# All-rows work of layer 0 gathered in two gaps of each tile

## The chip, the cores and the metric

The kernel runs on one core of a Trainium2 chip. The metric is the device time of one execution in microseconds (us); the kernel before takes 2685.39 us (median of 3 runs, 2684.89 to 2687.76). All times below are in us. The engines are TensorE (PE; PEld are its weight loads), VectorE (DVE), ScalarE (ACT), GpSimd (POOL) and the queue that starts transfers (SP).

## The reference, cut to what matters

The input x is 4 images of 128 channels and 64 x 64 positions, in float32. Two layers run over the N = 4096 positions of each image:

```
# layer 0: attention without a mask, heads of 64 channels for q and k
xf = group_norm(x).reshape(b, 128, N)
q = Wq @ xf + bq;  k = Wk @ xf + bk;  v = Wv @ xf + bv      # q, k: 64 x N, v: 128 x N
x = x + v @ softmax(q.T @ k).T
# layer 1: causal attention over tokens, then a recurrent network
t = tokens(x);  u = layer_norm(t)
t = t + softmax(causal(u Wq.T (u Wk.T).T / sqrt(128))) (u Wv.T)
t = t + ffn(layer_norm(t))
```

The ffn projects with W, normalises over all tokens and runs a recurrence through time. The change doesn't touch it.

## The kernel before

An image is called a batch in the code (B = 4). Its 4096 query positions form NQ = 8 tiles of QT = 512. All batches go one after the other; in each, the 8 tiles of layer 0 come first, then the 8 tiles of layer 1. A tile is worked off in units. A unit is 256 key positions, as two halves of 128, against the tile's 512 queries. A tile of layer 0 has 16 units; tile c of layer 1 has 2(c + 1), since later keys are masked.

A unit has three parts. `score` (L408) multiplies K by Q on TensorE into a PSUM pair `ps` (L428) and takes the exponential on ScalarE into `s` (L441), or, for the first unit of a tile, straight into `total`, which the profile calls `tot`. `product` (L443) multiplies `s` by V on TensorE and accumulates in PSUM, `av` (L457), and adds `s` to `total` on VectorE (L475). The loop at L496 issues the scores of unit i + 1, then a `turn` of queued jobs, then the products of unit i. TensorE so has the exponential of one unit to wait for while it does the scores of the next.

In layer 0, q and k have 64 rows. K and Q are stored twice, in rows 0 to 63 and 64 to 127, and the two halves of a unit run side by side in two halves of the TensorE array. The products too are split into two sums of 64 rows each, `av0` and `av1`. The profile shows such matmuls as 64*128. Layer 1 and all other work use all 128 rows (128*128). "All-rows work" below means matmuls of 128 rows that are put between the units of layer 0. They are:

- `pq` of `prep0` (L317): the projection that gives Q of the next tile, copied out by ScalarE (L321);
- `pz` of `end` (L361): a matmul with `blocks` that sums, over partitions, the `part` that VectorE has made of `total` (L351 to L356). Its reciprocal (L363) and a transpose on VectorE (L365) scale the products (L367), and X is updated (L370);
- `pt` and `pb` of `layernorm` (L157): four transposes of a finished tile of X (L161), copied out by ScalarE (L163), statistics on VectorE (L167, L169), a power on GpSimd (L155), normalisation on VectorE into the V of layer 1 (L174), and four transposes back (L180), copied into the K of layer 1 (L181);
- `pq` and `pz`, `pm`, `px` of `prep1` and `sample` (L338, L234): Q of the first tile of layer 1, and one sampled score per batch that sets the shift of the exponential.

When a tile of layer 0 or the last of layer 1 is done, its sums are copied out of PSUM (`acc`, L469: one half by ScalarE, one by VectorE), and the next tile's first product waits for these copies, for its `av` uses the same banks.

What runs between the units is decided by a list of jobs. A job is a generator that yields between its steps; `turn` (L225) makes one step of each of the first two jobs. `end` of a tile and `prep` of the next are put at the head, norms and the norms and projections for the ffn (`wx`, L383: `pt_f`, `pb_f`, `pw`) at the tail. In layer 0 this gives, per tile, a gap with `pq` and `pz`, one with `pt` and one with `pb`, each two units after the one before. The norm of tile c is queued as soon as X of that tile is updated, and so runs in tile c + 1. A part of the last tile's work runs in the first units of layer 1. The order on each engine is that in which instructions are issued, with small shifts: on VectorE the sums of a tile stand ahead of the copy of `acc`.

PSUM for all-rows work comes from `ps_m`, two buffers that are used in turn. `s` tiles come from `sp`, four buffers.

Of the kernel before, what the change touches and what calls it, by code (L numbers as in the profile page):

```python
# [64 lines left out]
def fast(  # L65
# [13 lines left out]
    NQ = N // QT  # L79
# [110 lines left out]
    def residual(b, tag):  # L190

        T[b] = kv.tile([P, N], F32, tag=tag, name=f"T_{b}")
        nc.sync.dma_start(out=T[b], in_=D[b])

    with ExitStack() as actx:
# [22 lines left out]
        jobs = deque()  # L218

        def queue(steps):  # L220
            job = Job(steps)
            jobs.append(job)
            return job
# [8 lines left out]
        norms, ends, preps, feeds = {}, {}, {}, {}  # L232
# [93 lines left out]
        def norm1(b, c):  # L326

            if c == 0:
                K[1, b] = kv.tile([P, N], F32, tag="K1", name=f"K1_{b}")
                V[1, b] = kv.tile([P, NB, C], F32, tag="V1", name=f"V1_{b}")  # L330
            yield from layernorm(
                X[:, b, ts(c, QT)], tmp, small, ps_m, f"1_{b}_{c}",
                V[1, b][:, 4 * c : 4 * c + 4, :], K[1, b][:, ts(c, QT)],
            )
            if c == 0:
                preps[1, b, 0] = queue(prep1(b, 0))

        def prep1(b, c):  # L338
            pq = ps_m.tile([P, QT], F32, tag="m", name=f"pq1_{b}_{c}")
            nc.tensor.matmul(pq, lhsT=A1, rhs=K[1, b][:, ts(c, QT)], start=True, stop=True)  # L340
            Q[1, b, c] = qp.tile([P, QT], F32, tag="q1", name=f"q1_{b}_{c}")
            nc.scalar.copy(Q[1, b, c], pq)
            yield
            if c == 0:
                yield from sample(1, b)

        def end(layer, b, c, av, total):

            name = f"{layer}_{b}_{c}"
            both = total[:, 0, :]  # L350
            nc.vector.tensor_tensor(both, both, total[:, 1, :], ALU.add)  # L351

            zt = tmp.tile([P, QT // R, R], F32, tag="zt", name=f"zt_{name}")
            nc.vector.transpose(zt.rearrange("p j a -> p (j a)"), both)  # L354
            part = small.tile([P, QT // R], F32, tag="part", name=f"part_{name}")
            nc.vector.tensor_reduce(part, zt, AX.X, ALU.add)  # L356
            if len(av) == 2:
                nc.vector.tensor_tensor(av[0], av[0], av[1], ALU.add)
            yield
            pz = ps_m.tile([P, QT // R], F32, tag="m", name=f"pz_{name}")  # L360
            nc.tensor.matmul(pz, lhsT=blocks, rhs=part, start=True, stop=True)  # L361
            r = sums[:, (layer * B + b) * NQ + c, :]
            nc.vector.reciprocal(r, pz)  # L363
            rt = tmp.tile([P, QT], F32, tag="rt", name=f"rt_{name}")
            nc.vector.transpose(rt.rearrange("p (j a) -> p j a", a=R), r.unsqueeze(2).to_broadcast([P, QT // R, R]))  # L365
            u = one.tile([P, QT], F32, tag="u", name=f"u_{name}")
            nc.vector.tensor_tensor(u, av[0], rt, ALU.mult)  # L367
            dst = X[:, b, ts(c, QT)]
            if layer == 0:
                nc.vector.scalar_tensor_tensor(dst, u, gn[b]["bv"], dst, ALU.add, ALU.add)  # L370
                norms[b, c] = queue(norm1(b, c))
                yield
                return
            yield
            yield
            po = ps_m.tile([P, QT], F32, tag="m", name=f"po_{name}")
            nc.tensor.matmul(po, lhsT=W1v, rhs=u, start=True, stop=True)  # L377
            nc.vector.tensor_tensor(dst, dst, po, ALU.add)  # L378
            nc.sync.dma_start(out=D[b][:, ts(c, QT)], in_=dst)
            queue(wx(b, c))  # L380
            yield
# [16 lines left out]
        units = []  # L398
# [9 lines left out]
        def score(i):  # L408
            layer, b, c, u, n = units[i]
            t = layer, b, c  # L410
            if u == 0:
                if layer == 0 and c == 0:
                    for job in feeds[b]:
                        job.complete()
                if layer == 1:
                    ends[0, b, c].complete()
                    norms[b, c].complete()
                if t not in preps:
                    preps[t] = queue((prep1 if layer else prep0)(b, c))
                preps[t].complete()  # L420
                totals[t] = tot.tile([P, 2, QT], F32, tag="total", name=f"tot_{layer}_{b}_{c}")
            s = totals[t] if u == 0 else sp.tile([P, 2, QT], F32, tag="s", name=f"s_{i}")
            exps[i] = s
            first = [columns(layer, c, u, h) for h in range(2)]
            ps = ps_pair.tile([P, 2, QT], F32, tag="pair", name=f"ps_{i}")
            for h in range(2):
                rows = slice(0, P) if layer else ds(h * CQ, CQ)
                nc.tensor.matmul(  # L428
                    ps[:, h, first[h] :], lhsT=K[layer, b][rows, ts(2 * u + h, P)],
                    rhs=Q[t][rows, first[h] :], start=True, stop=True,  # L430
                )
            if layer and u >= 2 * c:
                for h in range(2):
                    edge = ps[:, h, ds(first[h], P)]
                    nc.vector.tensor_tensor(edge, edge, mask, ALU.add)  # L435
                if u == 0:
                    nc.gpsimd.memset(s[:, 1, : first[1]], 0.0)
            for a in [(slice(None), slice(0, QT))] if first[1] == 0 else [
                (h, slice(first[h], QT)) for h in range(2)
            ]:  # L440
                nc.scalar.activation(s[:, *a], ps[:, *a], AF.Exp, bias=shift[layer, b])  # L441

        def product(i):  # L443
            layer, b, c, u, n = units[i]
            t = layer, b, c

            halves = [slice(0, P)] if layer else [ds(k * CQ, CQ) for k in range(2)]
            if u == 0:
                avs[t] = [
                    ps_av.tile([P, QT], F32, tag=f"av{(c + k) % 2}", name=f"av{k}_{layer}_{b}_{c}")  # L450
                    for k in range(len(halves))
                ]
            s, total, av = exps.pop(i), totals[t], avs[t]
            first = [columns(layer, c, u, h) for h in range(2)]
            for h in range(2):
                for rows, acc in zip(halves, av):
                    nc.tensor.matmul(  # L457
                        acc[:, first[h] :], lhsT=V[layer, b][rows, 2 * u + h, :],
                        rhs=s[rows, h, first[h] :],
                        start=u == 0 and h == 0, stop=u == n - 1 and h == 1,  # L460
                    )
            if u == n - 1 and (layer == 0 or c == NQ - 1):

                acc = [
                    pool.tile([P, QT], F32, tag=f"acc{k}", name=f"acc{k}_{i}")
                    for k, pool in zip(range(len(av)), (tmp, one))
                ]
                for cp, dst, src in zip((nc.scalar.copy, nc.vector.tensor_copy), acc, av):
                    cp(dst, src)  # L469
                av = acc  # L470
            if u:
                for a in [(slice(None), slice(0, QT))] if first[1] == 0 else [
                    (h, slice(first[h], QT)) for h in range(2)
                ]:
                    nc.vector.tensor_tensor(total[:, *a], total[:, *a], s[:, *a], ALU.add)  # L475
            if u == n - 1:
                ends[t] = Job(end(layer, b, c, av, total))
                jobs.appendleft(ends[t])
            if u == 0:
                if layer == 1 and c == 3 and b + 1 < B:  # L480
                    start_batch(b + 1)
                if layer == 1 and c == 3 and b == B - 1:
                    residual(0, "K0")
                    residual(1, "V0")
                following = layer, b, c + 1
                if c + 1 < NQ and (layer == 0 or (b, c + 1) in norms and norms[b, c + 1].done):
                    preps[following] = Job((prep1 if layer else prep0)(b, c + 1))
                    jobs.appendleft(preps[following])

        def start_batch(b):  # L490
            feeds[b] = []
# [4 lines left out]
        for i in range(len(units)):  # L496
            if i + 1 < len(units):
                score(i + 1)
            turn()
            product(i)  # L500
        ends[1, B - 1, NQ - 1].complete()
# [545 lines left out]
```

## Time and profile before

| | before |
|---|---|
| median time | 2685.39 us |
| span of the profiled execution | 2683.1 us |
| busy: PE, DVE, ACT, POOL | 97%, 56%, 42%, 4% |
| matmuls of `av<-s` (L457) | 4864, mean 588 ns |
| matmuls of `ps` (L428) | 3200, mean 579 ns |
| `pq` of layer 0 (L319) | 64 matmuls, mean 640 ns |
| `pt`, `pb` for layer 1 (L161, L180) | 128 matmuls each, mean 285 ns |
| `pz` of `end` (L361), both layers | 128 matmuls, mean 225 ns |
| normalisation (L174), power (L155) | 342 ns on DVE, about 1007 ns on POOL |

A line of the timeline gives the start in us, the time to the end of the last of the merged instructions, engine, line and operation, the tile written and the tiles read, shapes, and how many instructions are merged. What stands in brackets is the idle time ahead of it and what ended it. In float32 a matmul appears as two passes, so that 4 `ps` rows are the two halves of a unit. Matmuls overlap and their ends are modelled: differences between starts tell more than durations.

### The profile page before, as it was taken

How to read it: one execution, taken by the hardware profiler on the slowest of the kernel's cores; microseconds unless marked ns; L12 is line 12 of the kernel's file. 1: busy time of each engine (PE TensorE's matmuls, PEld its weight loads, DVE VectorE, ACT ScalarE, POOL GpSimd, SP SyncE). 2: the span in 40 equal slices, each digit the busy share in tenths (PEclk: the TensorE clock that was granted, in tenths of full speed). 3: DMA queues.
4: the chain of work that ended last, by engine and by line, in shares of the span. 5: the costliest groups of instructions: out<-in, count | busy, mean ns of one | idle time of the engine just before them, and what ended most of it. 6: DMA issues, size and time to landing. Idle time of an engine off the chain costs nothing.

```text
span 2683.1 us, 25668 instructions
## 1 busy us (share of the span) xinstructions
PE 2598.7 (97%) x9970; PEld 1226.6 (46%) x9970; DVE 1497.6 (56%) x2552; ACT 1118.0 (42%) x1302; POOL 110.9 (4%) x130
## 2 busy tenths in 40 slices
PE   6999999999999999999999999999999999999974
PEld 3444444445444444454444444544544444454443
DVE  4565656544555556553556565654455656555466
ACT  3444443333444444333444444334344444333353
POOL 0000000000000000000000000000000000000005
PEclk9999999999999999999999999999999999999987
DMA  3000000000000000000000000000000000100013
GB/s 133 1 1 1 1 0 12 8 5 4 5 1 1 1 1 5 12 4 9 4 1 1 1 1 1 12 8 4 5 4 1 1 0 1 67 12 8 4 67 127
DMA packets 9234, 35.81 MB, mean 13 GB/s; under 512 B 2192, under 2 KB 2960, under 8 KB 7056
## 3 DMA queue, kind: packets, MB, share of 16 engines
q1 hardware_dynamic: 6912, 33.56, 3.2%
q8 instruction: 80, 1.31, 0.2%
q10 hardware_dynamic: 2192, 0.53, 0.1%
q14 instruction: 50, 0.41, 0.0%
HBM read 17.30 MB, written 16.78 MB: 13 GB/s over the span
## 4 chain that ended last, share of the span: by engine, by line
PE 89%; DVE 7%; ACT 1%; issue 1%; DMA 0%; POOL 0%; ACTq 0%; DVEq 0%; POOLq 0%
PE av L457 47%; PE ps L428 31%; DVE tot L475 2%; DVE pg L545 1%; PE pq L319 1%; ACT s L441 1%; PE pv L313 1%; PE pk L308 1%; PE po L377 1%; PE pq L340 1%; PE pw L389 1%; DVE zt L354 1%; DVE tot L351 1%; DVE part L356 1%; PE pt L161 1%
## 5 line engine op out<-in xcount | busy, mean ns | idle before, releaser
L457 PE MATMUL av<-s,V 64*128 64x512 f32 (+3 forms) x4864 | 1361.9, 588 | 0.0
L441 ACT ACTIVATE s<-ps,shift 128x1024 f32<-128x1024 f32 (+4 forms) x796 | 808.4, 1023 | 1316.2 <-PE ps L428 1174.2
L475 DVE TENSOR_TENSOR tot<-tot,s 128x1024 f32<-128x1024 f32 (+4 forms) x796 | 878.7, 1109 | 855.5 <-ACT s L441 733.0
L428 PE MATMUL ps<-q,K 64*128 64x512 f32 (+4 forms) x3200 | 1029.3, 579 | 0.0
L457 PEld LDWEIGHTS av<-s,V 64*128 64x128 f32 (+1 forms) x4864 | 547.2, 188 | 592.3 <-issue 584.9
L428 PEld LDWEIGHTS ps<-q,K 64*128 64x128 f32 (+1 forms) x3200 | 417.0, 189 | 481.8 <-issue 470.7
L457 PE MATMUL av<-tot,V 64*128 64x512 f32 (+2 forms) x384 | 123.0, 603 | 6.1 <-DVE acc L469 5.8
L441 ACT ACTIVATE tot<-ps,shift 128x1024 f32<-128x1024 f32 (+2 forms) x68 | 71.4, 1057 | 104.3 <-PE ps L428 84.1
L155 POOL TENSOR_TENSOR rstd<-rstd,mhalf 128x4 f32<-128x4 f32 x32 | 32.2, 1007 | 1441.5 <-DVE rstd L154 1441.5
L457 PEld LDWEIGHTS av<-tot,V 64*128 64x128 f32 (+1 forms) x384 | 49.0, 188 | 70.0 <-issue 38.5
L155 POOL TENSOR_TENSOR rstd_f<-rstd_f,mhalf 128x4 f32<-128x4 f32 x32 | 33.4, 1045 | 915.3 <-DVE rstd_f L154 915.3
L543 PE MATMUL pg<-Y,FV 128*128 128x256 f32 x208 | 53.3, 418 | 16.6 <-ACT Y L546 10.0
L435 DVE TENSOR_TENSOR ps<-ps,mask 128x128 f32<-128x128 f32 x128 | 38.0, 297 | 33.8 <-PE ps L428 31.5
L174 DVE TENSOR_SCALAR V<-xt,mv,rstd 128x128 f32<-128x128 f32 x128 | 36.0, 342 | 34.4 <-POOL rstd L155 34.4
L174 DVE TENSOR_SCALAR rows<-xt_f,mv_f,rstd_f 128x128 f32<-128x128 f32 x128 | 36.7, 342 | 31.2 <-POOL rstd_f L155 31.2
L546 ACT ACTIVATE Y<-pg,bias 128x256 f32<-128x256 f32 x104 | 45.8, 474 | 18.5 <-DVE pg L545 17.9
L543 PEld LDWEIGHTS pg<-Y,FV 128*128 128x128 f32 x208 | 36.7, 205 | 34.3 <-ACT Y L546 16.9
L545 DVE SCALAR_TENSOR_TENSOR pg<-X,gain,pg 128x256 f32<-128x256 f32 x108 | 48.2, 491 | 6.9 <-PE pg L543 6.6
L354 DVE STREAM_TRANSPOSE zt<-tot 128x512 f32<-128x512 f32 x64 | 45.5, 710 | 2.1
L378 DVE TENSOR_TENSOR X<-X,po 128x512 f32<-128x512 f32 x32 | 22.0, 688 | 42.7 <-PE po L377 42.7
L351 DVE TENSOR_TENSOR tot<-tot 128x512 f32<-128x512 f32 x64 | 44.3, 692 | 2.2
L365 DVE STREAM_TRANSPOSE rt<-sums 128x512 f32<-128x512 f32 x64 | 45.0, 703 | 0.6
(127 smaller groups left out, 1133.6 us busy)
## 6 DMA issues: line engine op xcount, KB each, us to landing
X<-in_x SPq DMA_DIRECT2D x8, 1024.0 KB, 7.3
D<-X SPq DMA_DIRECT2D x32, 256.0 KB, 2.0
T<-D SPq DMA_DIRECT2D x4, 2048.0 KB, 7.8
out<-T SPq DMA_DIRECT2D x4, 2048.0 KB, 13.5
W0k<-in_w0k ACTq DMA_DIRECT2D x2, 32.0 KB, 5.1
W0q<-in_w0q ACTq DMA_DIRECT2D x2, 32.0 KB, 4.8
W0v<-in_w0v ACTq DMA_DIRECT2D x1, 64.0 KB, 5.3
W1q<-in_w1q ACTq DMA_DIRECT2D x1, 64.0 KB, 7.3
```

Of the source, the lines that this page charges most:

```text
L155: nc.gpsimd.tensor_tensor(dst, dst, mhalf[:, :n], ALU.pow)
L174: nc.vector.tensor_scalar(rows[:, j, :], xt[:, j, :], mv[:, j, 0:1], rstd[:, j : j + 1], ALU.subtract, ALU.mult)
L351: nc.vector.tensor_tensor(both, both, total[:, 1, :], ALU.add)
L354: nc.vector.transpose(zt.rearrange("p j a -> p (j a)"), both)
L365: nc.vector.transpose(rt.rearrange("p (j a) -> p j a", a=R), r.unsqueeze(2).to_broadcast([P, QT // R, R]))
L428: nc.tensor.matmul(ps[:, h, first[h] :], lhsT=K[layer, b][rows, ts(2 * u + h, P)], rhs=Q[t][rows, first[h] :], start=True, stop=True,)
L441: nc.scalar.activation(s[:, *a], ps[:, *a], AF.Exp, bias=shift[layer, b])
L457: nc.tensor.matmul(acc[:, first[h] :], lhsT=V[layer, b][rows, 2 * u + h, :], rhs=s[rows, h, first[h] :], start=u == 0 and h == 0, stop=u = ...
L475: nc.vector.tensor_tensor(total[:, *a], total[:, *a], s[:, *a], ALU.add)
L543: nc.tensor.matmul(ps, lhsT=FV, rhs=last[:, b, :], start=True, stop=True)
L545: nc.vector.scalar_tensor_tensor(pv, wx, gain, pv, ALU.mult, ALU.add)
L546: nc.scalar.activation(y, ps, AF.Sigmoid, bias=bias)
```

## The change

All-rows work leaves the two-half layout of the array and comes back to it. The change gathers it in two gaps of each layer-0 tile. A new function `gap` is called ahead of `turn` in each unit of layer 0. At unit 0 it runs all of `prep0` for the next tile and the first step of the norm of the tile two back (`pq`, `pt`). At unit 2 it makes the norm's VectorE step. At unit 4 it runs the rest of `end` of the tile before (`pz`) and the last step of the norm (`pb`). Job handling follows:

- norms are made as jobs but not queued, except that of the last tile of a batch. That of the last but one is queued at the first tile of layer 1;
- the first step of `end`, which is VectorE work alone, is made at once in layer 0, and `end` is queued only in layer 1 and for the last tile of layer 0;
- `prep1` of tile 0 is queued at unit 8 of the last tile of layer 0, and no longer after the norm of tile 0.

```diff
@@ norm1
-            if c == 0:
-                preps[1, b, 0] = queue(prep1(b, 0))
@@ end
             if layer == 0:
                 nc.vector.scalar_tensor_tensor(dst, u, gn[b]["bv"], dst, ALU.add, ALU.add)
-                norms[b, c] = queue(norm1(b, c))
-                yield
+                norms[b, c] = Job(norm1(b, c))
+                if c == NQ - 1:
+                    jobs.append(norms[b, c])
                 return
@@ product
             if u == n - 1:
                 ends[t] = Job(end(layer, b, c, av, total))
-                jobs.appendleft(ends[t])
+                if layer == 0:
+                    ends[t].step()
+                if layer == 1 or c == NQ - 1:
+                    jobs.appendleft(ends[t])
             if u == 0:
...
+                if layer == 1 and c == 0:
+                    jobs.append(norms[b, NQ - 2])
                 following = layer, b, c + 1
-                if c + 1 < NQ and (layer == 0 or (b, c + 1) in norms and norms[b, c + 1].done):
-                    preps[following] = Job((prep1 if layer else prep0)(b, c + 1))
+                if layer == 1 and c + 1 < NQ and norms[b, c + 1].done:
+                    preps[following] = Job(prep1(b, c + 1))
                     jobs.appendleft(preps[following])
+
+        def gap(b, c, u):
+
+
+            norm = norms.get((b, c - 2))
+            if u == 0:
+                if c + 1 < NQ:
+                    preps[0, b, c + 1] = Job(prep0(b, c + 1))
+                    preps[0, b, c + 1].complete()
+                if norm:
+                    norm.step()
+            if u == 2 and norm:
+                norm.step()
+            if u == 4:
+                if c:
+                    ends[0, b, c - 1].complete()
+                if norm:
+                    norm.complete()
+            if u == 8 and c == NQ - 1:
+                preps[1, b, 0] = queue(prep1(b, 0))
@@ main loop
                 score(i + 1)
+            layer, b, c, u, n = units[i]
+            if layer == 0:
+                gap(b, c, u)
             turn()
             product(i)
```

## The prediction

> **What bounds the kernel now.** I read the page's busy times and its chain of waits first.
>
> ```profile
> PE 2598.7 (97%) x9970; PEld 1226.6 (46%) x9970; DVE 1497.6 (56%) x2552; ACT 1118.0 (42%) x1302; POOL 110.9 (4%) x130
> ...
> PE 89%; DVE 7%; ACT 1%; issue 1%; DMA 0%; POOL 0%; ACTq 0%; DVEq 0%; POOLq 0%
> PE av L457 47%; PE ps L428 31%; DVE tot L475 2%; DVE pg L545 1%; PE pq L319 1%; ACT s L441 1%; PE pv L313 1%; PE pk L308 1%; PE po L377 1%; PE pq L340 1%; PE pw L389 1%; DVE zt L354 1%; DVE tot L351 1%; DVE part L356 1%; PE pt L161 1%
> ```
>
> TensorE holds 89% of the chain; VectorE (56% busy) and ScalarE (42%) have room. So the change is priced in TensorE's own time, from the timeline of TensorE at a layer-0 tile change:
>
> ```profile
> 184.85 1.02 PE L428 MATMUL ps<-q,K 64*128 64x512 f32 x4
> 186.08 1.99 PE L457 MATMUL av<-tot,V 64*128 64x512 f32 x8 [0.21 <-DVE acc L469]
> 187.88 1.05 PE L428 MATMUL ps<-q,K 64*128 64x512 f32 x4
> 188.86 1.13 PE L319 MATMUL pq<-X,wq 128*128 128x512 f32 x2
> 189.82 0.29 PE L361 MATMUL pz<-part,blocks 128*128 128x16 f32 x2
> ...
> 191.86 1.03 PE L428 MATMUL ps<-q,K 64*128 64x512 f32 x4
> ...
> 194.44 1.02 PE L428 MATMUL ps<-q,K 64*128 64x512 f32 x4
> 195.39 0.66 PE L161 MATMUL pt<-ident,X 128*128 128x128 f32 x4
> ...
> 197.80 1.03 PE L428 MATMUL ps<-q,K 64*128 64x512 f32 x4
> ...
> 200.38 1.02 PE L428 MATMUL ps<-q,K 64*128 64x512 f32 x4
> 201.33 0.66 PE L180 MATMUL pb<-ident,V 128*128 128x128 f32 x4
> ...
> 203.74 1.02 PE L428 MATMUL ps<-q,K 64*128 64x512 f32 x4
> ```
>
> Each ps row begins a unit. Undisturbed units (191.86 to 194.44, 197.80 to 200.38) last 2.58, others nearby 2.57; I use 2.57. What a unit takes beyond that is the price of what lies in it: tile change 187.88 - 184.85 - 2.57 = 0.46 (the first product waits for L469's copies of the old sums); pq with pz 191.86 - 187.88 - 2.57 = 1.41; pt 0.79; pb 0.79. Elsewhere pq and pz stand alone:
>
> ```profile
> 113.62 1.02 PE L428 MATMUL ps<-q,K 64*128 64x512 f32 x4
> 114.57 1.13 PE L340 MATMUL pq<-K,A 128*128 128x512 f32 x2
> ...
> 117.45 1.02 PE L428 MATMUL ps<-q,K 64*128 64x512 f32 x4
> ```
>
> ```profile
> 366.41 1.05 PE L428 MATMUL ps<-q,K 64*128 64x512 f32 x4
> 367.39 0.40 PE L361 MATMUL pz<-part,blocks 128*128 128x16 f32 x2
> ...
> 369.54 1.02 PE L428 MATMUL ps<-q,K 64*128 64x512 f32 x4
> ```
>
> So pq alone costs 1.26 and pz alone 0.56. A pq is two passes of 512 columns. One pass takes 2.57/6 = 0.43 (a unit is twelve matmuls that run in pairs), so 0.86 is work and 0.40 is the way out of the two-half array and back. pt is 0.43 of work (four steps of 0.11) and 0.36 of that way. In layer 1, where every matmul is full size, the way is absent:
>
> ```profile
> 462.04 1.02 PE L377 MATMUL po<-u,W1v 128*128 128x512 f32 x2
> 462.90 0.60 PE L180 MATMUL pb<-ident,V 128*128 128x128 f32 x4
> 463.34 1.88 PE L457 MATMUL av<-s,V 128*128 128x512 f32 x4
> ```
>
> Four transposes behind po cost 463.34 - 462.90 = 0.44.
>
> **What the Trainium skill says.** "TensorEngine Tiling (Array Packing)", Key Properties: changing the tiling mode, not just the tile, drains TensorE. It gives no price; the trace agrees and prices it at 0.36 to 0.40 a gap. "TensorE: Matmul & The Clock Gate", Architectural detail: ScalarE and VectorE are strict FIFO. The trace agrees: VectorE stands 1.19 at L174 for GpSimd's power although sums are queued behind. "Perfetto Trace Analysis", Identifying the Most-Contended Engine: matmul busy time is a bad metric since matmuls are pipelined. Hence starts, not the 97%.
>
> **The change part by part**, from the order in which the two built programs put instructions on each engine.
>
> *Removed in layer 0, batches 1 to 3, each.* Seven tile changes at 0.46: 3.22. A first product's wait: 683.56 - 680.88 - 2.57 = 0.11. Seven pq+pz at 1.41: 9.87. Six pt at 0.79: 4.74. The last pt, which also waits 0.87 for X (L370): 373.84 - 369.54 - 2.57 = 1.73. Seven pb: 5.53. One pz: 0.56. Sum 25.76.
>
> *Put in their place.* Two pq alone 2.52; two pz alone 1.12; five pq+pt; one pt alone 0.79; six pz+pb. No row shows such pairs in layer 0. Bounds: they share one drain (1.26 + 0.43 = 1.69 and 0.56 + 0.43 = 0.99), or nothing is shared (1.26 + 0.79 = 2.05 and 1.35). I take sharing: pq+pz costs 1.41 where apart they cost 1.82, and po+pb adds 0.44. Then 8.45 and 5.94; sum 18.82. The tile-change wait is counted at nothing: the gap now stands in front of the first product, and 0.79 or more of all-rows work covers 0.46 (L469's copies are queued in the same places as before).
>
> *Moved.* pt and pb of tile 6 go into layer 1, without a drain: 0.87.
>
> *New waits at the layer change.* The last end now runs at once and pt of tile 7 comes right behind the scores that start at 412.36. Row by row on VectorE (before: mask at 411.50 for 0.29, then sums, end): reciprocal 0.26, transpose 0.71, a sum 0.35, u 0.69, a sum 0.30, X 0.75, with small gaps, reach about 414.9. TensorE comes there at about 414.3 (0.21 later than before, for pz). Wait about 0.8; bounds 0 and 3.3 (VectorE in the order of before wrote X only at 417.63). Behind pt stand the products and scores of layer 1's second tile, and nothing on TensorE can pass; on VectorE, L174 of this norm waits for the power with the sum and mask of unit 132 behind it, about 0.8 before its exponential is needed. Farther on, pt_f of tiles 0 and 1 share a gap, so VectorE does both norms together: rows of the second are ready at about 477.5 on the clock of before, TensorE wants them at 476.9. Wait about 0.7; bounds 0 and 1.5. Together 1.5 a batch.
>
> *Sum.* 25.76 - 18.82 - 0.87 - 1.5 = 4.57; three batches 13.7. Batch 0 before: no first wait, its first pq alone: 25.76 - 0.11 - 1.41 + 1.26 = 25.50. After, there is one pz less and its first pq falls where TensorE waits for the first exponential anyway (0.34 idle at 50.45), so it costs 0.5 instead of 1.26: 18.82 - 0.56 - 0.76 = 17.50. With 0.87 and 1.5 it saves 5.63. In all 19.3: 2685.4 - 19.3 = 2666.
>
> *At nothing.* The norm's statistics, power and L174 move ahead of the new tile's first sum on VectorE. Counted from the start of unit 1's scores: ScalarE has done exponential (1.11), q (0.69) and xt (0.58) at 3.5; then statistics 1.23, 0.17, GpSimd 1.0, L174 1.11 and the sum 1.23, which with gaps ends at about 8.4. The buffer it frees is wanted by unit 5's exponential (sp has 4), whose scores end at 0.86 + 1.69 + 1.72 + 3 x 2.57 + 0.86 = 12.8. ScalarE's copies end before the next exponential. pz's part is five units old. Sampling and every feed stay as they are.
>
> **Rivals.** (a) No shared drain: 11 pairs of 0.36, four batches: 15.8 lost, 2682. pq+pz speaks against it. (b) The tile-change wait remains, 28 x 0.46 = 12.9 lost: 2679. Against: the copies end at 185.94, and the first product would start past 187. (c) Both waits at the layer change at their upper bounds, 4.8 instead of 1.5: 4 x 3.3 = 13.2, 2679. For it: VectorE's dense stretch from 405 to 418. (d) No new wait: 6 less, 2660. (e) Slower: VectorE's early norm delays freeing of s, so that exponentials and scores stop some 1.5 in each of 24 gaps: 36 lost, 2702. Against: the 4.4 of room just worked out.
>
> **How the numbers follow.** Forecast 72%, (d) 8%, (c) 9%, (b) 4%, (a) 3%, (e) 4%. The range runs from 2659, just under (d), to 2677, which takes in waits of up to 4.2 a batch; (a), (b), (e) and the far end of (c) are left out, two in ten at most. 0.2% is 5.4: faster means under 2680. Forecast, (b), (c) and (d) lie there: 0.93; (a) is the same: 0.03; (e) slower: 0.04.
>
> **What would show it.** Layer 0 has about 19 to 24 gaps a batch (before 26 to 30). A ps-to-ps step of about 4.26 holds pq+pt, one of 3.56 pz+pb, and no bare step of 3.03 remains at a tile change. pt of tile 7 waits under 1 for L370's X. It is wrong if a pair costs above 2 or 1.3, if L457 still waits for L469, or if the wait at the layer change exceeds 3.

## The result and the profile after

The changed kernel takes 2661.78 us (median of 4 runs, 2661.63 to 2664.72), the kernel before 2685.47 beside it (4 runs): a ratio of 0.9913 [0.9896, 0.993], 23.7 us less. The profiled spans are 2659.9 and 2683.1. Lines have moved: L457 is now L456, L428 L427, L475 L474, L361 L359, L370 L368, L377 L376, L469 L468, L435 L434.

The page's busy times and its chain, after:

```profile
PE 2583.6 (97%) x9970; PEld 1219.6 (46%) x9970; DVE 1500.9 (56%) x2552; ACT 1118.2 (42%) x1302; POOL 110.5 (4%) x130
...
PE 95%; DVE 3%; DMA 0%; issue 0%; ACT 0%; POOL 0%; ACTq 0%; POOLq 0%; DVEq 0%
PE av L456 51%; PE ps L427 33%; DVE pg L572 1%; PE pq L319 1%; PE pv L313 1%; PE pk L308 1%; PE po L376 1%; PE pq L338 1%; PE pw L388 1%; DVE T L577 1%; PE pt L161 1%; PE pt_f L161 1%; PE pb L180 1%; PE pz L359 1%; PE pb_f L180 1%
```

The number of instructions of each kind is the same. VectorE's part of the chain falls from 7% to 3%, and its sums (L475 before) are gone from the list. The waits of TensorE say which link went. Before, this list had

```profile
PE av L457 <- DVE acc L469: 5.8, 28, 0.2
...
PE pt L161 <- DVE X L370: 3.5, 4, 0.9
```

(total us, times, longest). After, the list has neither of them; of what is left in it nothing is new (one wait of pt_f, 0.8 in both, is put down to another row). The 28 waits stood there with 0.21 each, but a tile change cost 0.45 from one ps row to the next: the idle time is only that part of the hole in which no modelled matmul runs. For the same reason a short wait need not stand in this list at all: pt of tile 7 still waits 0.28 for X, as the fourth experiment shows. The timeline of TensorE over a layer-0 tile change, after:

```profile
178.81 1.02 PE L427 MATMUL ps<-q,K 64*128 64x512 f32 x4
179.77 1.13 PE L319 MATMUL pq<-X,wq 128*128 128x512 f32 x2
180.73 0.60 PE L161 MATMUL pt<-ident,X 128*128 128x128 f32 x4
...
183.08 1.02 PE L427 MATMUL ps<-q,K 64*128 64x512 f32 x4
...
190.81 1.02 PE L427 MATMUL ps<-q,K 64*128 64x512 f32 x4
191.76 0.40 PE L359 MATMUL pz<-part,blocks 128*128 128x16 f32 x2
192.00 0.63 PE L180 MATMUL pb<-ident,V 128*128 128x128 f32 x4
...
194.39 1.02 PE L427 MATMUL ps<-q,K 64*128 64x512 f32 x4
```

183.08 - 178.81 = 4.27 holds pq, pt and the tile change; less a unit of 2.57 that is 1.70. 194.39 - 190.81 = 3.58 holds pz and pb: 1.01. These are also the medians over all such gaps of the trace (20 and 24). Lone ones cost 1.26 (pq), 0.79 (pt, pb) and 0.53 (pz).

Sums of unit starts (from the first ps of one stretch to the first of the next) place the whole gain:

| us | before | after | difference |
|---|---|---|---|
| layer 0 of batch 0 | 359.15 | 351.50 | -7.65 |
| layer 0 of batch 1 | 362.21 | 355.52 | -6.69 |
| layer 1 of batch 1 | 273.36 | 274.52 | +1.16 |

Batches 2 and 3 are as batch 1. In all -7.65 - 3 x 6.69 + 4 x 1.16 = -23.1; the spans differ by 23.2.

### The profile page after: what moved, and what is told of

The parts are those of the page before. It is cut to its first block, busy times and chain, and to the rows that moved or that the text cites. A ratio compares the mean times of both kernels' runs of the same rounds, so it can differ in the third digit from the quotient of the medians.

```text
span 2659.9 us, 25680 instructions
## 1 busy us (share of the span) xinstructions
PE 2583.6 (97%) x9970; PEld 1219.6 (46%) x9970; DVE 1500.9 (56%) x2552; ACT 1118.2 (42%) x1302; POOL 110.5 (4%) x130
## 4 chain that ended last, share of the span: by engine, by line
PE 95%; DVE 3%; DMA 0%; issue 0%; ACT 0%; POOL 0%; ACTq 0%; POOLq 0%; DVEq 0%
PE av L456 51%; PE ps L427 33%; DVE pg L572 1%; PE pq L319 1%; PE pv L313 1%; PE pk L308 1%; PE po L376 1%; PE pq L338 1%; PE pw L388 1%; DVE T L577 1%; PE pt L161 1%; PE pt_f L161 1%; PE pb L180 1%; PE pz L359 1%; PE pb_f L180 1%
## 5 line engine op out<-in xcount | busy, mean ns | idle before, releaser
L456 PE MATMUL av<-s,V 64*128 64x512 f32 (+3 forms) x4864 | 1355.2, 585 | 0.0
L474 DVE TENSOR_TENSOR tot<-tot,s 128x1024 f32<-128x1024 f32 (+4 forms) x796 | 880.2, 1111 | 796.4 <-ACT s L440 711.5
L427 PE MATMUL ps<-q,K 64*128 64x512 f32 (+4 forms) x3200 | 1027.9, 578 | 0.0
L456 PEld LDWEIGHTS av<-s,V 64*128 64x128 f32 (+1 forms) x4864 | 550.6, 188 | 611.5 <-issue 604.7
L427 PEld LDWEIGHTS ps<-q,K 64*128 64x128 f32 (+1 forms) x3200 | 414.0, 188 | 484.8 <-issue 473.6
L456 PE MATMUL av<-tot,V 64*128 64x512 f32 (+2 forms) x384 | 123.2, 606 | 0.0
L456 PEld LDWEIGHTS av<-tot,V 64*128 64x128 f32 (+1 forms) x384 | 45.7, 187 | 51.5 <-issue 49.8
L434 DVE TENSOR_TENSOR ps<-ps,mask 128x128 f32<-128x128 f32 x128 | 37.8, 295 | 33.0 <-PE ps L427 30.7
L167 DVE BATCH_NORM_STATS2 st<-xt 128x6 f32<-128x128 f32 x128 | 27.9, 280 | 34.6 <-ACT xt L163 34.6
L363 DVE STREAM_TRANSPOSE rt<-sums 128x512 f32<-128x512 f32 x64 | 45.4, 709 | 1.5
L377 DVE TENSOR_TENSOR X<-X,po 128x512 f32<-128x512 f32 x32 | 22.0, 687 | 42.7 <-PE po L376 42.7
```

The costliest lines, as they stand in the source:

```text
L427: nc.tensor.matmul(ps[:, h, first[h] :], lhsT=K[layer, b][rows, ts(2 * u + h, P)], rhs=Q[t][rows, first[h] :], start=True, stop=True,)
L456: nc.tensor.matmul(acc[:, first[h] :], lhsT=V[layer, b][rows, 2 * u + h, :], rhs=s[rows, h, first[h] :], start=u == 0 and h == 0, stop=u = ...
```

## Experiments

The theory to be tested: all-rows work that shares a gap saves the way out of the two-half array and back (0.36 to 0.40 a gap), and a filled tile change hides the wait for the copies of the old sums (0.45 each). Its rivals: D, that the shared way is all of it; W, that the tile-change wait is all of it. The first four kernels were timed beside each other and 30 runs of the kernel before (2685.17). Cuts in the edits are marked with three dots.

**The gaps one unit later.** Sharing stays, the tile change is empty again.

```diff
-            if u == 0:
+            if u == 1:
...
-            if u == 2 and norm:
+            if u == 3 and norm:
...
-            if u == 4:
+            if u == 5:
```

Expected: 

> Both gaps one unit later (units 1, 3 and 5 in place of 0, 2 and 4): the same gaps with the same work in them, but none at the tile change. My theory (drains saved, and the tile-change wait covered): the wait of 0.46 comes back at 28 tile changes, 12.9, less about 1 where the first projection of a batch now shares a gap with the sums, plus 0.75 where batch 0's first projection no longer falls in a wait: about 2674. Rival D (only the number of drains counts, the place of a gap doesn't): no change from the changed kernel, 2661 to 2662. Rival W (only the filled wait counts): about 2675.

Measured: 2676.18 (2675.06 to 2676.9, 6 runs), ratio 0.9964 [0.9952, 0.9977]: 14.4 more than the changed kernel. Its timeline at the tile change:

```profile
181.31 1.02 PE L427 MATMUL ps<-q,K 64*128 64x512 f32 x4
182.54 1.99 PE L456 MATMUL av<-tot,V 64*128 64x512 f32 x8 [0.21 <-DVE acc L468]
184.33 1.05 PE L427 MATMUL ps<-q,K 64*128 64x512 f32 x4
...
188.63 1.02 PE L427 MATMUL ps<-q,K 64*128 64x512 f32 x4
```

The pair still costs 188.63 - 184.33 - 2.57 = 1.73, and the bare step is back: 184.33 - 181.31 - 2.57 = 0.45, with the wait for L468 in brackets. The two together, per tile, are 0.48 more than the filled change. From the first scores of the program to the last, the trace is 12.9 longer than that of the changed kernel (3.96 in batch 0, 2.99 in each other), close to what the terms of the expectation add up to (12.9 - 1 + 0.75); the rest of the 14.4 lies ahead of the first scores and behind the last, where the edit changes nothing. D falls; W is not told apart by this run.

**The partners apart.** The tile change stays filled, but by pq alone.

```diff
                     preps[0, b, c + 1].complete()
-                if norm:
-                    norm.step()
+            if u == 1 and norm:
+                norm.step()
...
                     ends[0, b, c - 1].complete()
-                if norm:
-                    norm.complete()
+            if u == 5 and norm:
+                norm.complete()
```

Expected: 

> The changed kernel with the transposes one unit after the projection and one unit after the sums, so that no pair shares a way out of the two-half array. My theory: 11 pairs a batch pay 0.36 each, 15.8, and the last tile's change has no work in it any more, 4 x 0.46: about 2679. A step from scores to scores holds 3.83 for a lone projection, 3.13 for lone sums, 3.36 for lone transposes. Rival D: about 2678. Rival W (the way out costs nothing as such, the wait is all): only the last tiles' 1.8, about 2664.

Measured: 2678.39 (2677.53 to 2680.04, 9 runs), ratio 0.9974 [0.9964, 0.9984]: 16.6 more than the changed kernel. Its timeline, with pq and pt one unit apart and no wait at the tile change:

```profile
179.39 1.02 PE L427 MATMUL ps<-q,K 64*128 64x512 f32 x4
180.35 1.13 PE L319 MATMUL pq<-X,wq 128*128 128x512 f32 x2
...
183.22 1.02 PE L427 MATMUL ps<-q,K 64*128 64x512 f32 x4
184.18 0.66 PE L161 MATMUL pt<-ident,X 128*128 128x128 f32 x4
...
186.59 1.02 PE L427 MATMUL ps<-q,K 64*128 64x512 f32 x4
```

1.26 and 0.80 sum to 2.06 as against 1.70 together: 0.36 for one more way out and back. pz and pb apart cost 0.53 + 0.79 = 1.32 as against 1.01: 0.31. There are 11 more gaps a batch (35 instead of 24 in layer 0 of batch 1), five of the first kind and six of the second, and the change to the last tile, which only pt had filled, is empty again: 5 x 0.36 + 6 x 0.31 + 0.46 = 4.1 a batch, 16.5 of the 16.6. W falls.

The two losses add up to more than the gain, chiefly because the kernel before shared a gap already: pq with pz, 27 times at 1.26 + 0.53 - 1.42 = 0.37, which the change gives up. So the gain of a batch (5.53 in batches 1 to 3) is made of filled tile changes 7 x 0.45 = 3.2, new pairs 3.7 less lost pairs 7 x 0.37 = 2.6, the transposes of tile 6 moved to layer 1, where no way is paid, 2 x 0.79 - 0.88 = 0.7, and a shorter wait of tile 7's pt for X, 0.94 - 0.28 = 0.7: 5.7 by these rounded prices. The new partners alone bring 1.1 more than the old ones; what they allow is that the tile change is filled without giving that up.

**Only the projection moved, in the kernel before.**

```diff
+                yield
                 norms[b, c] = queue(norm1(b, c))
-                yield
...
-                if c + 1 < NQ and (layer == 0 or (b, c + 1) in norms and norms[b, c + 1].done):
-                    preps[following] = Job((prep1 if layer else prep0)(b, c + 1))
+                if layer == 1 and c + 1 < NQ and (b, c + 1) in norms and norms[b, c + 1].done:
+                    preps[following] = Job(prep1(b, c + 1))
...
+            if layer == 0 and u == 0 and c + 1 < NQ:
+                preps[0, b, c + 1] = Job(prep0(b, c + 1))
+                preps[0, b, c + 1].complete()
             turn()
```

The `yield` of `end` now stands ahead of the line that queues the norm, so the norm starts one turn later, and pz, pt and pb stay in gaps of their own. Expected: 

> The kernel before with one part of the change: the projection of the next tile stands in the tile change, in front of the first product; sums and transposes keep gaps of their own at units 2, 4 and 6 of the tile (norms wait one turn longer, so that transposes keep their distance from the sums). My theory: a tile pays 1.26 + 0.56 in place of 0.46 + 1.41, that is 0.05 less, 24 times; batch starts lose 0.25 three times, batch 0's first projection gains 0.75, and the last tile's transposes no longer wait 0.94 for X, four times: about 2680. Rival D (27 gaps more, 0.40 each, nothing for the place): about 2693. Rival W (wait filled at 27 changes, gaps free): about 2669.

Measured: 2680.36 (2679.2 to 2683.04, 20 runs), ratio 0.9983 [0.9976, 0.9989]. Its timeline at the tile change:

```profile
185.28 1.02 PE L428 MATMUL ps<-q,K 64*128 64x512 f32 x4
186.24 1.13 PE L319 MATMUL pq<-X,wq 128*128 128x512 f32 x2
...
189.12 1.02 PE L428 MATMUL ps<-q,K 64*128 64x512 f32 x4
190.07 0.40 PE L361 MATMUL pz<-part,blocks 128*128 128x16 f32 x2
...
192.22 1.02 PE L428 MATMUL ps<-q,K 64*128 64x512 f32 x4
```

The tile change with pq and the lone pz cost 1.27 and 0.53, where before the empty change and the pair cost 0.46 and 1.41: 1.80 as against 1.87. What the wait gave, the lone pz took back. Most of the 4.8 us comes from elsewhere: in batch 1, unit starts lose 0.35 at the first tile, where pq and pz are now apart, gain 0.08 at each of six later ones, and gain 0.94 at the last tile, where pt comes later and no longer waits for X. All three terms, and so the total, are near what was expected (0.25, 0.05 and 0.94); D and W are off by 13 and 11. Filling the tile change brings next to nothing (0.08) when it breaks a pair.

**The norm of tile 6 ahead of that of tile 7.** This takes away the wait of tile 7's pt for X, the disputed cost at the layer change.

```diff
@@ end
-                if c == NQ - 1:
-                    jobs.append(norms[b, c])
@@ product
                     jobs.append(norms[b, NQ - 2])
+                    jobs.append(norms[b, NQ - 1])
```

Expected: 

> The changed kernel with the norm of tile 6 ahead of that of tile 7 in layer 1. If the transposes of tile 7 wait for X at the layer change as the trace shows (about 0.27), the wait goes: 4 x 0.27 = 1.1 less, about 2660.7, and the step there shortens from 2.2 by 0.27. Rival: another wait of VectorE takes its place and the time stays at 2661.8 or rises.

Measured: 2660.96 (2660.19 to 2662.01, 4 runs), ratio 0.9908 [0.9891, 0.9924]. The times alone do not separate it from the changed kernel; the starts do: 0.28 earlier at unit 131 of each batch, 1.11 in all, and no other change above 0.03. The timeline of TensorE at the layer change, first of the changed kernel, then of this one:

```profile
405.32 1.88 PE L427 MATMUL ps<-q,K 128*128 128x512 f32 x4
407.26 0.66 PE L161 MATMUL pt<-ident,X 128*128 128x128 f32 x4
...
408.41 1.88 PE L427 MATMUL ps<-q,K 128*128 128x512 f32 x4
```

```profile
406.05 1.88 PE L425 MATMUL ps<-q,K 128*128 128x512 f32 x4
407.77 0.60 PE L161 MATMUL pt<-ident,X 128*128 128x128 f32 x4
...
408.86 1.88 PE L425 MATMUL ps<-q,K 128*128 128x512 f32 x4
```

pt comes 1.94 after the scores with the wait and 1.72 without; the next scores come 3.09 and 2.81 after.

**Other partners.** If a gap costs 0.36 whatever is in it, fewer gaps should be faster still. These three kernels put the projection together with the end's pz, one gap for two tiles' work (pq+pz costs 1.39 in their traces), give pb of one norm and pt of the next a common gap, let the first projection of layer 1 share the last tile's gap with pz, and leave the norms from tile EARLY on to layer 1. They so differ in more than the number of gaps:

```diff
-            if u == 0:
+            if u == (1 if b and c == 0 else 0):
                 if c + 1 < NQ:
                     preps[0, b, c + 1] = Job(prep0(b, c + 1))
                     preps[0, b, c + 1].complete()
...
                 if c:
                     ends[0, b, c - 1].complete()
...
+            if u == 4:
+                if 2 <= c < EARLY + 2:
+                    norms[b, c - 2].complete()
+                if 1 <= c < EARLY + 1:
+                    norms[b, c - 1].step()
+            if u == 6 and 1 <= c < EARLY + 1:
+                norms[b, c - 1].step()
...
-                    jobs.append(norms[b, NQ - 2])
+                    jobs.extend(norms[b, k] for k in range(EARLY, NQ))
```

Expected, EARLY = 3: 

> As the kernel with four norms in layer 0, but with three there, five in layer 1. The gaps fall by 4 and 3 x 3, 5.2 less, but the norms of tiles 3 and 4 are not done when layer 1 wants to project them ahead, so their projections come right before the scores that need them, and TensorE waits for norm, projection and ScalarE's copy: eight such places at 1 to 3 each. Theory: 2661 to 2675, above the kernel with four. Rival (only drains count): 2656.

Expected, EARLY = 4: 

> A further step: the sums go into the tile change with the projection (one way out instead of two), the norms of tiles 0 to 3 stay in layer 0, one tile behind, with the transposes of two tiles paired at unit 4, and the norms of tiles 4 to 7 go to layer 1, where transposes pay no way out; the projection of layer 1's first tile joins the last tile's change. Three gaps a batch fewer than in the changed kernel (16 to 19 in batch 0, 21 to 24 after): 12 x 0.40 = 4.8, and the wait of 0.28 for X at the layer change goes, 1.1. Theory: about 2656. Rival: layer 1's first tiles are full, and waits for VectorE take the place of the drains: 2662 or more.

Expected, EARLY = 5: 

> As the kernel of the same call with four norms in layer 0, but with five there. Two gaps fewer than the changed kernel in batch 0, one in each later batch: 5 x 0.40 = 2.0, and 1.1 for the wait for X: about 2659. Rival as for four norms: 2662 or more.

Measured beside 9 runs of the kernel before (2685.26), with the gaps and the time of batch 1 (200 units) from the traces; each has the same matmuls in it. Only a gap in layer 0 pays the way, so its gaps stand in brackets:

| kernel | median us (runs) | ratio | gaps (in layer 0) | batch, us |
|---|---|---|---|---|
| changed kernel | 2661.78 (4) | 0.9913 [0.9896, 0.993] | 73 (24) | 630.04 |
| EARLY = 3 | 2658.21 (4) | 0.9902 [0.9887, 0.9917] | 66 (21) | 628.92 |
| EARLY = 4 | 2664.15 (5) | 0.9924 [0.991, 0.9937] | 68 (21) | 631.13 |
| EARLY = 5 | 2658.42 (4) | 0.9897 [0.9882, 0.9912] | 69 (23) | 628.45 |

EARLY = 5 came out as expected, EARLY = 4 missed by 8, and EARLY = 3 was better than the waits feared for it and nearer its rival, that only the ways count. The medians of 3 and 5 lie 3.6 and 3.4 under the changed kernel, every run of them under its fastest, though in another session and with overlapping intervals. The batch times, which repeat within 0.03 from batch 1 to batch 2 of a trace, agree: 1.1 and 1.6 less. The number of gaps in layer 0 does not order these kernels: 21 is both the second fastest batch and the slowest. The miss of EARLY = 4 shows in the first tile of the next batch, into which work of layer 1 (po, pt_f, pb_f, pw) spills. TensorE's timeline there:

```profile
1308.11 1.12 PE L455 MATMUL av<-s,V 64*128 64x512 f32 x2
1309.17 1.12 PE L387 MATMUL pw<-cols,FW 128*128 128x512 f32 x2
1310.22 1.55 PE L455 MATMUL av<-s,V 64*128 64x512 f32 x5
1311.19 0.59 PE L426 MATMUL ps<-q,K 64*128 64x512 f32 x1
1311.61 0.59 PE L455 MATMUL av<-s,V 64*128 64x512 f32 x1
1311.62 1.01 PE L426 MATMUL ps<-q,K 64*128 64x512 f32 x2
...
1313.77 0.59 PE L426 MATMUL ps<-q,K 64*128 64x512 f32 x1
1314.19 0.59 PE L455 MATMUL av<-s,V 64*128 64x512 f32 x1
1314.19 1.44 PE L426 MATMUL ps<-q,K 64*128 64x512 f32 x3
1315.57 1.12 PE L375 MATMUL po<-u,W1v 128*128 128x512 f32 x2
```

pw falls between the products of a unit and so pays a way of its own (0.40). It also splits them unevenly: the two passes ahead of it start one after the other (1308.11 and 1308.65) where passes of the two halves start together, so they are of one half and run without a partner. That half then stays ahead, and scores of one half run beside products of the other. As long as both have work this costs nothing: 1313.77 - 1311.19 = 2.58 is a bare unit. The cost shows where the halves come together again: ahead of po the half that is behind has its last two passes to do alone (the last two of the three ps rows from 1314.19, at 1314.62 and 1315.05), and that unit costs 0.85 more than the same one with EARLY = 5 (2.11 as against 1.26, po in both): two passes of 0.43. Two gaps later (at 1328.35), eight transposes pb_f take 1.72 where eight pt_f take 1.09. The first ten units hold 10.8 beyond bare units as against 6.8 with EARLY = 5; work of 1.7 (eight transposes at 0.11 and one pw at 0.86) is in that, so some 2.3 a batch is lost by order and waits, 6.9 in the three batches that follow another. About 1.9 of the 2.3 is in the three steps named (0.40 for the way, 0.85, and 0.63 for the transposes); for the rest, and for why the order came out so, no run was made.

## Why the prediction was right, and where it fell short

- *The prices.* pq+pt was put at 1.69 and measured 1.70; pz+pb 0.99 and 1.01; no bare step of 3.03 remains at a tile change. The partners apart cost 16.6, the empty tile change 14.4 (12.9 by unit starts). Both mechanisms are shown, and rivals (a) and (b) are out. The Trainium skill, "TensorEngine Tiling (Array Packing)", Key Properties, says that a change of the tiling mode drains TensorE; the runs agree in that a way out and back has a price, 0.31 to 0.40 here, and add that full-array work pays it per gap, not per piece.
- *Layer 0.* Forecast 25.50 - 17.50 = 8.00 in batch 0 and 25.76 - 18.82 = 6.94 in the others; measured 7.65 and 6.69. Two terms hold most of the 0.25 to 0.35. Six pz+pb at 1.01 and not 0.99 are 0.12. And the first projection of a batch costs 1.37 and not 1.26, so that the first product's wait of 0.11, counted as removed, is still paid; in batch 0 it saves 0.61 (0.72 + 1.26 before, 1.37 after) and not 0.76.
- *The moved transposes.* 0.87 forecast; 1.16 less the wait of 0.28 is 0.88.
- *New waits at the layer change: the term that was off.* "Together 1.5 a batch" was 0.28, so 4 x 1.22 = 4.9 was subtracted too much. Less the 1.1 that layer 0 fell short, that is 3.8, the difference of the forecast gain of 19.3 and the 23.1 of the unit starts. Part of it was in the working already: its own times give 414.9 - 414.3 and 477.5 - 476.9, 0.6 for each wait and not 0.8 and 0.7, and it names no reason for the rest. The range of 2659 to 2677 had room for an error of this size. Rival (c), larger waits, is out; (d), no wait, with 2660, was nearer than the forecast.

Why it was off can be read in VectorE's timeline at the layer change, after:

```profile
404.24 0.29 DVE L434 TENSOR_TENSOR ps<-ps,mask 128x128 f32<-128x128 f32 x1
404.44 0.25 DVE L361 RECIPROCAL sums<-pz 128x16 f32<-128x16 f32 x1
404.72 0.71 DVE L363 STREAM_TRANSPOSE rt<-sums 128x512 f32<-128x512 f32 x1
405.36 0.38 DVE L474 TENSOR_TENSOR tot<-tot,s 128x256 f32<-128x256 f32 x1
405.66 0.68 DVE L365 TENSOR_TENSOR u<-acc,rt 128x512 f32<-128x512 f32 x1
406.26 0.28 DVE L474 TENSOR_TENSOR tot<-tot,s 128x128 f32<-128x128 f32 x1
406.46 0.74 DVE L368 SCALAR_TENSOR_TENSOR X<-u,bv,X 128x512 f32<-128x512 f32 x1
```

The order is the one forecast, but in five of the six steps the next row starts 0.07 to 0.09 before the end of the one ahead of it (405.66 + 0.68 = 406.34, next start 406.26). The exception is the transpose, which reads what the reciprocal writes: it starts 0.03 after. The trace of before has the same two kinds of step. There the transpose zt (L354) starts 0.03 after the end of the L351 that it reads, 61 of 61 times, and a sum (L475) behind the reciprocal (L363), which it does not read, starts 0.04 to 0.09 before its end, 47 times. The end of tile 7 was for the most part a chain of the first kind before; the change lets sums stand between its links. X is there 2.96 after the mask starts; the forecast added up durations and small gaps to 3.4. Its own durations, 3.35 in all, less five overlaps of 0.08 and with one gap of 0.03, would have given an estimate of 2.98. The Trainium skill, "Perfetto Trace Analysis", Optimizing Scalar/DVE Operations, says that the write-acknowledgement half of an instruction's access overhead overlaps with the next instruction, and puts the busy overhead of VectorE on SBUF at about 60 ns; the trace agrees with 70 to 90 ns for rows that do not read each other, and not for those that do. The prediction should have drawn on it. The mask also lies 1.08 ahead of the scores and not 0.86, and TensorE arrives 1.72 after they start and not 1.94. The second wait, for the shared gap of pt_f and pb_f, is not there. VectorE and TensorE, after:

```profile
468.18 1.94 DVE L174 TENSOR_SCALAR rows<-xt_f,mv_f,rstd_f 128x128 f32<-128x128 f32 x7
468.20 1.88 PE L427 MATMUL ps<-q,K 128*128 128x512 f32 x4
...
469.92 1.04 PE L180 MATMUL pb_f<-ident,rows 128*128 128x128 f32 x8
```

Seven normalisations of 0.34 take 1.94, not 2.4, and the transposes start 1.72 after the scores, the same as pt without a wait: they begin with the first rows while the last ones are still being written (470.12). The forecast had wanted both norms complete.

- *At nothing.* VectorE's early norm delays nobody: no wait for it stands in the list of TensorE, and rival (e) is out.

## What to carry to other kernels

Where a kernel runs row-tiled, count the gaps in which it leaves that layout: each costs 0.3 to 0.4 us here whatever lies in it, so put full-array pieces together, and put one such gap where TensorE waits anyway. Let it fall where both halves have done the same work, and not between the products of a unit, as the one trace with such a gap shows. Test both together: filling the wait with a piece torn from its partner gave 0.08 us a tile. To find when a chain of VectorE instructions ends, add the steps between their starts in a like stretch, not their durations, and ask of each step whether the next instruction reads the one ahead of it.

## What was not expected of the hardware

- VectorE instructions that follow each other without a wait overlap by 0.07 to 0.09 us in the records where the second does not read the first, and stand 0.03 apart where it does (above). Seven of 0.34 step by 0.27.
- Scores of one half of the array ran beside products of the other at no cost (2.58 us for the unit). All-rows work put in while one half was two passes ahead cost two passes, 0.85 us (EARLY = 4). This was read from one trace; no run put it to the test.
- The first scores of the first batch began 0.72 us later in the profile of the swapped norms than in that of the changed kernel, ahead of anything that differs between them; a gain of 1.1 us can only be read from starts.
